# Reordering the opening of a cross-attention and feed-forward kernel: unit-matrix products first, transposes ahead of keys, small pieces between maxima

## The chip, the core and the metric

The kernel runs on one core of a Trainium2 chip. A core has five engines with a queue each: TensorE (matrix products into PSUM; PE in the profile, its weight loads PEld), VectorE (DVE), ScalarE (ACT), GpSimd (POOL) and SyncE (SP, which here only issues transfers). The metric is the time of one execution in microseconds (us) on the device. The kernel before was run three times: 1314.48, 1314.66 and 1316.01 us, median 1314.66. Its traced execution is a further one.

## What is computed

One cross-attention layer and one feed-forward layer, each with a residual. Tokens are 2048 x 256, the context 1601 x 192, 16 heads of 64. A learned null key and value stand ahead of the 1601 context keys, so there are 1602. Cut to what matters:

```python
def xattn(x, context, mask, g_norm, null_kv, Wq, Wkv, Wout, g_out):
    x = layer_norm(x, g_norm)
    q = x @ Wq
    k, v = jnp.split(context @ Wkv, 2, axis=-1)
    # heads split; null key and value put ahead of k and v
    sim = jnp.einsum('bhid,bhjd->bhij', q * sqrt_scale, k * sqrt_scale)
    sim = jnp.where(full_mask, sim, max_neg)
    attn = jax.nn.softmax(sim, axis=-1)
    out = jnp.einsum('bhij,bhjd->bhid', attn, v)
    return layer_norm(heads_joined(out) @ Wout, g_out)

x = x + xattn(layernorm(x), ctx_768, mask, ...)
x = x + ffn(layernorm(x), k0, k1, k2, s0, s1, s2)   # three layers with weights of +1 and -1
```

## The kernel before

Heads are taken in pairs (8 pairs, `p`), tokens in blocks of 512 (4 blocks, `b`); a unit is one pair and one block, and there are 32. A unit needs the queries of its block (`project_q`: `qT` for the scores, `qr` in a rounded format for the maxima), the keys of its pair (`kT`, `kr`), the values (`v`) and, for each query, the largest score over all keys. The maxima of the next unit are found while the exponentials of this one run. Keys are taken in three chunks of 512 and a rest of 66 (`CHUNKS`), tokens of a block in four tiles of 128; `max_chunk` number `3 * t + c` is token tile `t` against key chunk `c`, and number 12 (`REST`) is all four tiles against the rest. Each is a pair of products on TensorE (L338, one for each head; L322 for the rest) and a reduction on VectorE (L341; L325 for the rest).

`max_combined` (L346) joins the maxima of a unit into `mcol`, `max_turned` transposes that on TensorE (L351) and spreads it into `mT` on VectorE (L353). The first two score tiles of a unit add `mT` through a product with ones (L386), so that a unit's first exponential (L388) needs it. After its 13 exponentials a unit does the weighted sums (L395) and the projections for later units.

The change touches the opening (L506 to L550), all that runs ahead of unit 0. It is written out by hand: every engine executes its instructions in the order in which the code issues them. What it does:

- Transfers are issued from three queues: tokens, weights of pair 0 and context on SyncE and ScalarE; mask, null key, `g_norm` (as `gn_sb`) and small things on GpSimd. GpSimd also makes the unit matrix `ident`.
- Block 0 of the tokens is normed: statistics (L77, L78) and a square root (`input_root`), then four tiles scaled on VectorE (`input_normed`, L89).
- `first_keys(n)` projects a key chunk: two products (L214 with the first 128 context rows, L215 with the rest), then VectorE masks it into `kT` (L217) and rounds it into `kr` with the null key put in (L218).
- `input_turned(0)` transposes the normed tiles (eight transposes, L440) and multiplies by `gn_sb`: one half on ScalarE (L441), the other on VectorE (L445).
- Statistics of token block 1 are taken in two parts, around the VectorE work of key chunk 1. Block 1 is normed on ScalarE (`centred_beside`, eight activations), and then the table of the exponential is loaded (L523).
- `project_q(0, 0)`: four passes on TensorE (L203), copies on ScalarE (L204, L205).
- The maxima of unit 0 come in three rounds of four token tiles, one round for each of the key chunks 0, 1 and 2. Between them stand the key chunks 2 and 3, four groups of values (`first_values`, 4, 4, 4 and 1 tiles of 128 keys, two products of two passes each, one copy on ScalarE, L265) and the transposes of block 1.
- `keys_stepped` replaces each 256 keys by the difference to the 256 before, on GpSimd (L251).
- After the last maxima: `max_combined`, the query projection of block 1, `max_turned`.

In the opening, products go to PSUM slots that `slot` hands out, by turns from two pools (`spare` and `flex`) of two slots each. A tile takes over the slot of the tile four calls before it, and waits until that one has been read.

Of the kernel before, what the change touches and what calls it, by code (L numbers as in the profile page):

```python
# [30 lines left out]
REST = 12  # L31
# [5 lines left out]
def xattn_ffn(ctx, tc, x, ctxT, mask, g_norm, null_kv, wq, wkv, wout, g_out, k0, k1, k2, s0, s1, s2, out):  # L37
    nc = tc.nc
# [14 lines left out]
    x_sb = cp.tile([128, NB * 4, D], F32, name="x_sb")  # L53
# [7 lines left out]
    ident = cp.tile([128, 128], F32, name="ident")  # L61
    xnT = cp.tile([128, NB, 2, 512], F32, name="xnT")
# [25 lines left out]
    def centred(dst, src, mv, r, j):  # L88
        nc.vector.tensor_scalar(dst, src, mv[:, j, 0:1], r[:, j : j + 1], ALU.subtract, ALU.mult)  # L89
# [56 lines left out]
    with ExitStack() as att:  # L146
# [20 lines left out]
        weights = {}  # L167
# [26 lines left out]
                pp.tile([128, KEYS], F32R, tag="kr", name=f"kr_{p}"),  # L194
            )

        def project_q(p, b, get=flex):

            qT = wp.tile([128, 512], F32, tag="qT", name=f"qT_{p}_{b}")
            qr = wp.tile([128, 512], F32R, tag="qr", name=f"qr_{p}_{b}", bufs=1)  # L200
            ps = get(f"psq_{p}_{b}")
            for c in range(2):
                nc.tensor.matmul(ps[:, 0, :], weights[p][0][:, c, :], xnT[:, b, c, :], start=c == 0, stop=c == 1)  # L203
            nc.scalar.mul(qr, ps[:, 0, :], DH**-0.5)  # L204
            nc.scalar.mul(qT, ps[:, 0, :], DH**-0.5)  # L205
            queries[p, b] = (qT, qr)

        def first_keys(n, get):

            kT, _, kr = pairs[0]  # L210
            start, w = CHUNKS[n]
            keys = ds(start, w)
            ps = get(f"psk_0_{n}")
            nc.tensor.matmul(ps[:, 0, :w], weights[0][1][:, 0, :], ctx_a[:, keys], start=True, stop=False)  # L214
            nc.tensor.matmul(ps[:, 0, :w], weights[0][2][:, 0, :], ctx_b[:, keys], start=False, stop=True)  # L215

            nc.vector.tensor_tensor(kT[:, keys], ps[:, 0, :w], keep[:, keys], ALU.mult)  # L217
            nc.vector.scalar_tensor_tensor(kr[:, keys], drop[:, keys], nullk[:, 0:1], kT[:, keys], ALU.mult, ALU.add)  # L218
            if n == 0:
                nc.vector.tensor_copy(kT[:, 0:1], nullk)  # L220
# [25 lines left out]
        def keys_stepped(p):  # L246

            kT = pairs[p][0]
            for at in range(256 * ((KEYS - 1) // 256), 0, -256):
                w = min(256, KEYS - at)  # L250
                nc.gpsimd.tensor_tensor(kT[:, ds(at, w)], kT[:, ds(at, w)], kT[:, ds(at - 256, w)], ALU.subtract)  # L251

        def first_values(n, get):

            v = pairs[0][1]
            tiles = range(4 * n, min(4 * n + 4, KC))
            rows = 128 if n < 3 else KLAST
            ps = get(f"psv_0_{n}")
            for i, t in enumerate(tiles):
                keys = ds(128 * t, rows)  # L260
                out_t = ps[:rows, 0, ts(i, 128)]
                nc.tensor.matmul(out_t, ctx_a[:, keys], weights[0][1][:, 1, :], start=True, stop=False)
                nc.tensor.matmul(out_t, ctx_b[:, keys], weights[0][2][:, 1, :], start=False, stop=True)
            w = len(tiles)
            nc.scalar.copy(  # L265
                v[:rows, ds(4 * n, w), :], ps[:rows, 0, : 128 * w].rearrange("p (t d) -> p t d", d=128)
            )
            if n == 0:
                nc.gpsimd.tensor_copy(v[0:1, 0, :], nullv)
# [149 lines left out]

        def input_root(b, mv=None):
            mv = mv or stats(x_sb[:, ts(b, 4), :], 4, f"x{b}")
# [12 lines left out]
        def input_turned(b, get=flex):  # L436
            pt = get(f"xT_{b}")
            for j in range(4):
                for c in range(2):
                    nc.tensor.transpose(pt[:, c, ts(j, 128)], y_sb[:, 4 * b + j, ts(c, 128)], ident)  # L440
            nc.scalar.mul(xnT[:, b, 0, :], pt[:, 0, :], gn_sb[:, 0:1])  # L441
            if b == 1:
                nc.scalar.mul(xnT[:, b, 1, :], pt[:, 1, :], gn_sb[:, 1:2])
            else:
                nc.vector.tensor_scalar_mul(xnT[:, b, 1, :], pt[:, 1, :], gn_sb[:, 1:2])  # L445
# [63 lines left out]
        xn = input_root(0)  # L509

        for keys in (ds(0, 512), ds(512, KEYS - 512)):
            nc.scalar.activation(drop[:, keys], keep[:, keys], AF.Identity, bias=ones[:, 0:1], scale=-1.0)
        input_normed(0, *xn)
        first_keys(0, slot)
        input_turned(0, slot)
        mv = stats(x_sb[:, 4:6, :], 2, "x1")
        first_keys(1, slot)
        mv = stats(x_sb[:, 6:8, :], 2, "x1", mv)
        xn = input_root(1, mv)
        project_q(0, 0, slot)  # L520
        input_normed(1, *xn, beside=True)

        nc.scalar.activation(warm, eps_sb, AF.Exp)  # L523
        for t in range(4):
            max_chunk(0, 0, 3 * t, slot)
            if t == 1:
                first_keys(2, slot)
        for t in range(4):
            max_chunk(0, 0, 3 * t + 1, slot)
            if t == 0:  # L530
                first_keys(3, slot)
                keys_stepped(0)
            else:
                first_values(t - 1, slot) if t < 3 else input_turned(1, slot)

        nc.vector.tensor_scalar(maskb[:, : KC - 1], mcol_u8[:, : KC - 1], -MASKED, MASKED, ALU.mult, ALU.add)
        nc.vector.tensor_scalar(
            maskb[:KLAST, KC - 1 : KC], mcol_u8[:KLAST, KC - 1 : KC], -MASKED, MASKED, ALU.mult, ALU.add
        )
        for t in range(4):  # L540
            max_chunk(0, 0, 3 * t + 2, slot)
            if t == 0:
                max_chunk(0, 0, REST, slot)
            if t == 1:
                first_values(2, slot)
            if t == 2:
                first_values(3, slot)
        max_combined(0, 0)
        project_q(0, 1, flex)
        max_turned(0, 0)  # L550
        begin.__exit__(None, None, None)
        last = None
# [256 lines left out]
```

## Time and profile before

| what | value |
|---|---|
| median of three runs | 1314.66 us |
| the profiled execution | 1314.12 us |
| its span, first to last instruction | 1312.3 us |
| TensorE busy in it | 1288.0 us (98%) |
| VectorE busy | 820.1 us (62%) |
| ScalarE busy | 625.3 us (48%) |
| GpSimd busy | 998.9 us (76%) |
| mean granted TensorE clock | 0.993 |
| first reduction of a maximum starts | 20.45 us |
| last maxima joined (L346) starts | 41.58 us |
| `mT` (L353) starts | 43.14 us |
| first exponential (L388) starts | 44.43 us |

Times inside the profile are us from the start of the span. Busy time counts an engine's instructions, except register, branch, semaphore and transfer-issuing ones. An idle time in square brackets is followed by what ended it, inferred from semaphore events; "issue" is time for which the profile shows no such event. An fp32 product is two passes on TensorE, and the counts behind an "x" are passes. The ends of products are modelled, so the start of the next pass tells more than a duration. "PEclk" is the granted clock of TensorE as a share of full speed (on the page in tenths).

### The profile page before, as it was taken

To read this page: it belongs to the slowest core of one execution; us is meant where nothing else is said; L and a number is where in the kernel's file an instruction comes from. 1 tells how busy PE (TensorE), PEld (TensorE's weight loads), DVE (VectorE), ACT (ScalarE), POOL (GpSimd) and SP (SyncE) were. 2 spreads that over 40 slices of the span, in tenths; PEclk is the share of its full clock that TensorE was granted. 3 is DMA by queue.
4 is the path that set the end of the run, shared out by engine and by line. 5 is a ranking of instruction groups with operands and counts; after the bars stand their busy time and mean duration, and the time that the engine had idled before them with its cause. 6 is when DMAs were issued, how large, how long until landed. Compare 5 with 4: busy or idle time off the path is not lost.

```text
span 1312.3 us, 15885 instructions
## 1 busy us (share of the span) xinstructions
PE 1288.0 (98%) x6528; PEld 654.4 (50%) x6528; DVE 820.1 (62%) x822; ACT 625.3 (48%) x740; POOL 998.9 (76%) x503
## 2 busy tenths in 40 slices
PE   6989999999999999999999999999999999999998
PEld 3434444444444444444444444444444443688887
DVE  6877666666666666666666666666666784554431
ACT  3566444444444445455555555555555457421121
POOL 3578988898889888898889888988898999611100
PEclk8989999999999999999999999999999999999999
DMA  6100000000000000000000000000000010000000
GB/s 142 22 1 4 0 1 13 5 1 0 12 5 1 1 13 1 4 1 1 13 5 0 0 13 5 0 1 4 0 17 1 0 41 0 1 9 8 17 16 16
DMA packets 16121, 13.16 MB, mean 10 GB/s; under 512 B 2656, under 2 KB 15520, under 8 KB 16048
## 3 DMA queue, kind: packets, MB, share of 16 engines
q1 hardware_dynamic: 14928, 11.02, 3.2%
q8 instruction: 51, 0.84, 0.3%
q0 software_dynamic: 480, 0.34, 0.2%
q10 hardware_dynamic: 640, 0.79, 0.2%
q14 instruction: 22, 0.18, 0.0%
HBM read 10.04 MB, written 2.10 MB: 9 GB/s over the span
## 4 chain that ended last, share of the span: by engine, by line
PE 92%; DVE 3%; ACT 2%; POOL 2%; issue 1%; DVEq 0%; POOLq 0%; ACTq 0%
PE sT L375 28%; PE av L395 26%; PE ps L693 9%; PE max L338 7%; PE psq L203 4%; PE po L403 4%; PE ps L719 2%; PE den L413 2%; PE psv L280 2%; PE psk L228 1%; PE sT L386 1%; DVE mx L341 1%; POOL acc L596 1%; PE psv L292 1%; PE psk L233 1%; PE max L322 1%
## 5 line engine op out<-in xcount | busy, mean ns | idle before, releaser
L596 POOL TENSOR_TENSOR acc<-acc,e 128x1024 f32<-128x1024 f32 (+1 forms) x352 | 847.4, 2407 | 27.6
L341 DVE TENSOR_REDUCE mx<-max 128x2 f32<-128x1024 f32 x384 | 452.0, 1222 | 84.1 <-PE max L338 84.0
L388 ACT ACTIVATE e<-sT,maskb 128x1024 f32<-128x1024 f32 (+1 forms) x416 | 460.1, 1115 | 39.4 <-PE sT L386 8.8
L375 PE MATMUL sT<-qT,kT 64*128 64x512 f32 (+1 forms) x1664 | 449.6, 612 | 0.8 <-ACT e L388 0.2
L395 PE MATMUL av<-e,v 128*64 128x512 f32 (+1 forms) x1664 | 369.5, 594 | 0.2 <-ACT e L388 0.2
L338 PE MATMUL max<-kr,qr 64*128 64x512 f32 x768 | 292.3, 751 | 3.2 <-ACT qr L204 2.3
L395 PEld LDWEIGHTS av<-e,v 128*64 128x64 f32 (+1 forms) x1664 | 116.7, 137 | 237.7 <-issue 223.2
L375 PEld LDWEIGHTS sT<-qT,kT 64*128 64x128 f32 (+1 forms) x1664 | 130.7, 181 | 153.4 <-ACT e L388 144.4
L644 ACT COPY avs<-av 128x512 f32<-128x512 f32 x32 | 18.7, 586 | 321.6 <-PE av L395 321.6
L415 DVE RECIPROCAL aoT<-den 128x512 f32<-128x512 f32 x31 | 104.1, 3357 | 59.9 <-PE den L413 59.9
L594 POOL TENSOR_TENSOR acc<-e,e 128x1024 f32<-128x1024 f32 x32 | 75.6, 2363 | 71.0 <-ACT seen L584 57.8
L338 PEld LDWEIGHTS max<-kr,qr 64*128 64x128 f32 x768 | 76.3, 187 | 93.8 <-DVE mx L341 69.4
L353 DVE TENSOR_TENSOR mT<-mt,pick 128x512 fp32r<-128x512 f32 x32 | 22.1, 691 | 119.1 <-PE mt L351 119.1
L693 PE MATMUL ps<-h0hi,w 128*128 128x512 f32 x256 | 79.6, 392 | 0.1
L693 PE MATMUL ps<-h0lo,w 128*128 128x512 f32 x256 | 78.9, 389 | 0.0
L122 POOL TENSOR_TENSOR y_sb<-y_sb,gout_sb 128x256 f32<-128x256 f32 x12 | 9.3, 777 | 88.8 <-DVE y_sb L89 88.8
L204 ACT ACTIVATE qr<-psq 128x512 fp32r<-128x512 f32 x32 | 19.1, 597 | 97.4 <-PE psq L203 97.4
L203 PE MATMUL psq<-xnT,wq 128*128 128x512 f32 x128 | 62.0, 608 | 2.5 <-DVE xnT L445 2.5
L682 DVE SCALAR_TENSOR_TENSOR h1lo<-ps,h1hi 128x1024 fp32r<-128x1024 f32 x16 | 19.6, 1224 | 68.3 <-ACT h1hi L681 68.2
L681 ACT ACTIVATE h1hi<-ps 128x1024 fp32r<-128x1024 f32 x16 | 16.4, 1026 | 94.9 <-PE ps L693 94.9
L403 PE MATMUL po<-wo,aoT 128*128 128x256 f32 x256 | 60.6, 379 | 0.0
L251 POOL TENSOR_TENSOR kT<-kT 128x256 f32<-128x256 f32 (+1 forms) x48 | 31.8, 662 | 36.0 <-DVE kr L240 17.5
(153 smaller groups left out, 1075.6 us busy)
## 6 DMA issues: line engine op xcount, KB each, us to landing
out_x<-o SPq DMA_DIRECT2D x7, 256.0 KB, 2.1
x_sb<-in_x SPq DMA_DIRECT2D x3, 512.0 KB, 8.4
wa<-in_wkv SPq DMA_DIRECT2D x8, 128.0 KB, 2.7
wq<-in_wq SPq DMA_DIRECT2D x8, 128.0 KB, 2.2
wo<-in_wout SPq DMA_DIRECT2D x8, 128.0 KB, 2.1
xnT<-in_k SPq DMA_DIRECT2D x1, 1024.0 KB, 5.8
wb<-in_wkv SPq DMA_DIRECT2D x15, 64.0 KB, 2.4
ctx_a<-in_ctxT SPq DMA_DIRECT2D x2, 256.0 KB, 8.8
```

The lines of the kernel that those rows point to most:

```text
L203: nc.tensor.matmul(ps[:, 0, :], weights[p][0][:, c, :], xnT[:, b, c, :], start=c == 0, stop=c == 1)
L251: nc.gpsimd.tensor_tensor(kT[:, ds(at, w)], kT[:, ds(at, w)], kT[:, ds(at - 256, w)], ALU.subtract)
L338: nc.tensor.matmul(ps[:, j, :w], qr[rows, ts(t, 128)], kr[rows, ds(start, w)], start=True, stop=True)
L341: nc.vector.tensor_reduce(maxima[p, b][:, t, :, c], ps[:, :, :w], AX.X, ALU.max)
L375: nc.tensor.matmul(ps[:n, j, :], kT[rows, ds(128 * k, n)], qT[rows, :], start=k < 2, stop=k >= 2, skip_group_check=k >= 2,)
L388: nc.scalar.activation(e[:n], ps[:n], AF.Exp, bias=maskb[:n, k : k + 1])
L395: nc.tensor.matmul(av[ts(j, DH), 0, :], v[:n, k, ts(j, DH)], e[:n, j, :], start=k == 0, stop=k == KC - 1)
L403: nc.tensor.matmul(pv[:, t, :], aoT[:, ts(t, 128)], weights[p][3], start=True, stop=True)
L415: nc.vector.reciprocal(aoT, ps)
L594: nc.gpsimd.tensor_tensor(acc, es[0], es[1], ALU.add)
L596: nc.gpsimd.tensor_tensor(acc[:m], acc[:m], es[k][:m], ALU.add)
L693: nc.tensor.matmul(ps[:, f, :], w(c)[:, ts(2 * g + f, 128)], parts[part][:, c, :], start=i == 0, stop=i == len(steps) - 1,)
```

## The change

All of it is in the opening; the unit loop and the feed-forward part are as they were.

1. Behind the norming of block 0, twenty products of `ident` with itself go to a PSUM tile `idle` that nobody reads. They are the first work on TensorE.
2. The transposes of block 0 (`input_turned(0)`) come ahead of key chunk 0, the query projection of block 0 ahead of key chunk 1. On VectorE, L445 is thus ahead of the first keys.
3. The statistics of block 1 are no longer split: all four tiles are taken behind the first keys and ahead of the VectorE work of key chunk 1. `input_root` loses its second argument.
4. `first_values` takes a `part`: two of a group's four tiles in each call, the copy behind the second. `project_q` can be called in two parts, too, one product in each.
5. The maxima stand in the same three rounds, but between two of them at most one small piece is placed: half a group of values, a key chunk, the transposes of block 1, or half of the query projection of block 1. That projection now stands ahead of `max_combined`, its first half ahead of chunk 8 and its second behind chunk 11, and it takes its PSUM tile from `slot` instead of `flex`.

The order of TensorE's work from key chunk 1 on, before: max 0, 3, keys 2, max 6, 9, 1, keys 3, max 4, values 0, max 7, values 1, max 10, transposes of block 1, max 2, rest, 5, values 2, max 8, values 3, max 11, first scores, query 1, turned maxima. After: max 0, 3, keys 2, max 6, half of values 0, max 9, the other half, max 1, keys 3, half of values 1, max 4, the other half, max 7, transposes of block 1, max 10, half of values 2, max 2, the other half, rest, values 3, max 5, half of query 1, max 8, 11, the other half, first scores, turned maxima. The order of GpSimd's and SyncE's work and of all transfers is the same, but for the copy of the null value, which now stands ahead of `keys_stepped` on GpSimd.

```diff
-        def project_q(p, b, get=flex):
-
+        def project_q(p, b, get=flex, part=None):
+
+            if part is not None:
+                if part == 0:
+                    halves["q"] = get(f"psq_{p}_{b}")
+                ps = halves["q"]
+                nc.tensor.matmul(
+                    ps[:, 0, :], weights[p][0][:, part, :], xnT[:, b, part, :], start=part == 0, stop=part == 1
+                )
+                if part == 0:
+                    return
...
-        def first_values(n, get):
+        def first_values(n, part, get):
...
-            ps = get(f"psv_0_{n}")
+            if part == 0:
+                halves[n] = get(f"psv_0_{n}")
+            ps = halves[n]
             for i, t in enumerate(tiles):
+                if i // 2 != part:
+                    continue
...
             w = len(tiles)
+            if part == 0 and w > 1:
+                return
...
         input_normed(0, *xn)
+
+        idle = slot("idle")
+        for _ in range(20):
+            nc.tensor.matmul(idle[:, 0, :128], ident, ident, start=True, stop=True)
+        input_turned(0, slot)
         first_keys(0, slot)
-        input_turned(0, slot)
-        mv = stats(x_sb[:, 4:6, :], 2, "x1")
+        project_q(0, 0, slot)
+        xn = input_root(1)
         first_keys(1, slot)
-        mv = stats(x_sb[:, 6:8, :], 2, "x1", mv)
-        xn = input_root(1, mv)
-        project_q(0, 0, slot)
         input_normed(1, *xn, beside=True)
 
         nc.scalar.activation(warm, eps_sb, AF.Exp)
-        for t in range(4):
-            max_chunk(0, 0, 3 * t, slot)
-            if t == 1:
-                first_keys(2, slot)
-        for t in range(4):
-            max_chunk(0, 0, 3 * t + 1, slot)
-            if t == 0:
-                first_keys(3, slot)
-                keys_stepped(0)
-            else:
-                first_values(t - 1, slot) if t < 3 else input_turned(1, slot)
+
+        max_chunk(0, 0, 0, slot)
+        max_chunk(0, 0, 3, slot)
+        first_keys(2, slot)
+        max_chunk(0, 0, 6, slot)
+        first_values(0, 0, slot)
+        max_chunk(0, 0, 9, slot)
+        first_values(0, 1, slot)
+        max_chunk(0, 0, 1, slot)
+        first_keys(3, slot)
+        keys_stepped(0)
+        first_values(1, 0, slot)
+        max_chunk(0, 0, 4, slot)
+        first_values(1, 1, slot)
+        max_chunk(0, 0, 7, slot)
+        input_turned(1, slot)
+        max_chunk(0, 0, 10, slot)
...
-        for t in range(4):
-            max_chunk(0, 0, 3 * t + 2, slot)
-            if t == 0:
-                max_chunk(0, 0, REST, slot)
-            if t == 1:
-                first_values(2, slot)
-            if t == 2:
-                first_values(3, slot)
+        first_values(2, 0, slot)
+        max_chunk(0, 0, 2, slot)
+        first_values(2, 1, slot)
+        max_chunk(0, 0, REST, slot)
+        first_values(3, 0, slot)
+        max_chunk(0, 0, 5, slot)
+        project_q(0, 1, slot, 0)
+        max_chunk(0, 0, 8, slot)
+        max_chunk(0, 0, 11, slot)
+        project_q(0, 1, slot, 1)
         max_combined(0, 0)
-        project_q(0, 1, flex)
         max_turned(0, 0)
```

More of the change, by code (lines that the diff above doesn't have):

```diff
@@ L195, in open_pair @@
             )
-        def project_q(p, b, get=flex):
+        def project_q(p, b, get=flex, part=None):
[8 more added lines that the diff above has]
+                    return
             qT = wp.tile([128, 512], F32, tag="qT", name=f"qT_{p}_{b}")
             qr = wp.tile([128, 512], F32R, tag="qr", name=f"qr_{p}_{b}", bufs=1)
-            ps = get(f"psq_{p}_{b}")
-            for c in range(2):
+            if part is None:
+                ps = get(f"psq_{p}_{b}")
+            for c in range(2) if part is None else ():
                 nc.tensor.matmul(ps[:, 0, :], weights[p][0][:, c, :], xnT[:, b, c, :], start=c == 0, stop=c == 1)
@@ L251, in keys_stepped @@
                 nc.gpsimd.tensor_tensor(kT[:, ds(at, w)], kT[:, ds(at, w)], kT[:, ds(at - 256, w)], ALU.subtract)
-        def first_values(n, get):
+        halves = {}
+        def first_values(n, part, get):
             v = pairs[0][1]
@@ L417, in divided, with input_root @@
             return aoT
-        def input_root(b, mv=None):
-            mv = mv or stats(x_sb[:, ts(b, 4), :], 4, f"x{b}")
+        def input_root(b):
+            mv = stats(x_sb[:, ts(b, 4), :], 4, f"x{b}")
             r = sp.tile([128, 4], F32, tag="rstd", name=f"rstd_x{b}")
```

## The prediction

> **What bounds the kernel now.** First the page: the chain of work that ended last, followed back from the end, and the granted clock.
>
> ```profile
> PEclk8989999999999999999999999999999999999999
> PE 92%; DVE 3%; ACT 2%; POOL 2%; issue 1%; DVEq 0%; POOLq 0%; ACTq 0%
> ```
>
> Over the whole span TensorE sets the end. The change edits only the opening, and there another engine may bind, so the opening is read alone. It ends where the first shifts (mT, L353) let the first exponentials start, at 44.4 us. The table of busy time by stretch comes next (length, then busy us of PE, PEld, DVE, ACT, POOL, the clock, DMA share, GB/s).
>
> ```profile
> 20.45:41.58 21.13, 19.29 (x102) 13.04 (x101) 16.67 (x19) 8.29 (x16) 4.19 (x7) 0.84 0.08 16
> 41.58:44.43 2.85, 2.85 (x11) 1.20 (x11) 0.88 (x2) 1.09 (x3) 0.00 (x0) 1.00 0.89 200
> ```
>
> The first stretch runs from the first maximum to the last. VectorE has 16.67 us of work in 21.13 us: 4.46 us idle. VectorE's timeline says what it waited for.
>
> ```profile
> 12.39 0.69 DVE L217 TENSOR_TENSOR kT<-psk,keep 128x512 f32<-128x512 f32 x1 [3.64 <-issue]
> ...
> 14.76 0.75 DVE L445 TENSOR_SCALAR xnT<-xT,gn_sb 128x512 f32<-128x512 f32 x1 [0.64 <-ACT xnT L441]
> ...
> 20.45 2.36 DVE L341 TENSOR_REDUCE mx<-max 128x2 f32<-128x1024 f32 x2 [0.81 <-PE max L338]
> 23.95 0.69 DVE L217 TENSOR_TENSOR kT<-psk,keep 128x512 f32<-128x512 f32 x1 [1.15 <-PE psk L215]
> ...
> 31.91 1.23 DVE L341 TENSOR_REDUCE mx<-max 128x2 f32<-128x1024 f32 x1 [1.49 <-PE max L338]
> 34.33 1.23 DVE L341 TENSOR_REDUCE mx<-max 128x2 f32<-128x1024 f32 x1 [1.19 <-PE max L338]
> ...
> 41.58 0.19 DVE L346 TENSOR_REDUCE mcol<-mx 128x8 f32<-128x32 f32 x1
> 43.14 0.69 DVE L353 TENSOR_TENSOR mT<-mt,pick 128x512 fp32r<-128x512 f32 x1 [1.37 <-PE mt L351]
> ```
>
> Each idle stretch ends with a TensorE product that came late: a key chunk at 23.95, maxima at 31.91 and 34.33 that stood behind whole groups of values, the turned maxima at 43.14 that stood behind a query projection (40.94 to 42.76). Why TensorE was late is in the chain of the opening (start, us, what) and in its clock.
>
> ```profile
> 10.59 1.71 PE psk L215 x2
> ...
> 29.31 0.43 PE psv L263 x2
> ...
> 33.18 0.22 PE psv L263 x2
> 17.65:21.06 3.41, 1.16 (x5) 1.00 1.13 288
> 21.06:24.50 3.44, 3.44 (x8) 0.51 0.08 22
> 24.50:27.88 3.38, 1.80 (x13) 1.00 0.00 0
> 27.88:31.30 3.42, 3.42 (x16) 0.50 0.00 0
> ```
>
> The same two passes take 0.43 us at clock 0.5 and 0.22 us at 1.0. The clock fell at 21.06 and 27.88, after stretches in which TensorE was busy 1.16 and 1.80 of 3.4 us, and came back after stretches in which it was always busy. (The column reads 1.00 before 21 us, yet the key chunk at 10.59 takes 1.71 us where its like at 14.87 takes 0.86, so I go by durations there.)
>
> The last view is the landing of two transfers, issued at 3.68 and 5.46 us; the last number is us to landing.
>
> ```profile
> gn_sb<-in_g_norm POOLq DMA_DIRECT2D x1, 1.0 KB, 7.8
> x_sb<-in_x SPq DMA_DIRECT2D x1, 512.0 KB, 9.2
> ```
>
> So gn_sb lands at 11.5 (GpSimd's own wait on it ends at 11.79) and the second token block at 14.66. No transfer is moved by the change, so these times stand.
>
> **The change part by part.** *Unit-matrix products.* Twenty fp32 products of 128 columns wait for ident alone, which is ready at 2.64 us. A value tile's two products are four passes and take 0.43 us at half clock, so twenty take 20 x 0.215 = 4.3 us and end at 6.9. The transposes queued behind them need the first normed tile, at 7.38 + 0.41 = 7.8. The cover is 0.9 us; with twice the passes the burst would end near 11.2, the transposes at 12.9, and the loss would be about 1.1 us. What they gain I take as nothing: after the burst TensorE has eight transposes and one key chunk, then waits for gn_sb, so by 12 us it can be at half clock again, and nothing that the clock speeds up before 12 us is waited for.
>
> *Transposes ahead of keys.* They follow the normed tiles and end near 9.2 (before: 13.8). Their readers (L441 on ScalarE, L445 on VectorE) gain a new limit, gn_sb. I take GpSimd's 11.79 rather than 11.5: ScalarE then copies 11.8 to 12.5, VectorE starts at 12.5. Behind L445 on VectorE stand the first keys, the statistics of block 1 and all maxima; behind L441 on ScalarE stands qr. The first key chunk needs wb (issued 1.95, landing 7.6 us later, 9.55) and at half clock ends by 11.3; VectorE asks for it at 13.2: hidden. The query's second half starts at 13.25, ends by 14.1 at half clock, and key chunk 1 by 15.8; VectorE asks for it at 17.05: hidden. Key chunk 2 waits for its transfers (8.42 + 8.4 = 16.8), ends by 18.5, and is asked for at 20.9: hidden.
>
> *VectorE's queue, added up from 12.5.* L445 0.67 (14.76 to 15.43); first keys and null column 1.72 (12.39 to 14.11), which gives 14.89, past the landing at 14.66; four statistics of 0.54 (two take 15.43 to 16.51) give 17.05; keys 1, 1.36 (16.51 to 17.87), give 18.41; reciprocal and negated mean 0.24 (19.40 to 19.64) give 18.65. The first maximum, at 20.45 before, thus starts 1.8 us earlier. From there the work is the same 16.67 us: 35.3 if VectorE never waits, against 41.58.
>
> *Values, keys, queries between chunks.* The PSUM slots are four, taken in turn. A maximum costs VectorE 1.14 us (2.36 for two, overlapping). Between two maxima TensorE has one pair of products, 0.43 us, and one piece of some 0.43 us: 0.87 at full clock, inside 1.14; 1.3 to 1.7 at half clock, outside it. Two places are thin. The first copy of values stands on ScalarE behind eight norming steps and a table load (3.9 + 1.5 us, from 18.65 to 24.1), ends at 24.7 and frees the slot of the second values; the maximum behind them is ready by 26.0 and asked for at 26.25. Then eight transposes of block 1 (1.04 us at full clock, 1.7 at half) stand ahead of chunk 10: ready by 28.0 at full clock, 29.5 at half, asked for at 28.5. So VectorE waits 0 to 1 us there; if nothing improved it would keep all 4.46 us. I take 0.5, near the low end, since no whole group of values stands ahead of a maximum any more. [...]
>
> *Query 1 between the last chunks.* Half of it now stands ahead of chunk 8, the rest behind chunk 11, while VectorE still reduces. The turned maxima then wait for mcol alone: 0.19 + some 0.08 + 0.38 (42.76 to 43.14) = 0.65 us from L346 to L353, against 1.56: 0.9 saved.
>
> *Entry to unit 0.* TensorE is idle about 2 us of the last 3.4 before mT, so the clock may fall as it did at 21.06. A scoring step takes 1.17 us and holds 0.70 us of TensorE work (47.09 to 47.54 scores, 0.25 maxima): 1.4 at half clock, so three steps lose 0.7 us at most, 0 at least. I take 0.2.
>
> Sum: -1.8 - 4.46 + 0.5 - 0.91 + 0.2 = -6.5 us. The units behind it have no fixed time left to wait for (the last opening transfers land at about 20 us, and the reload of ctx_b follows the last values), so it reaches the end whole. The profiled execution took 1314.12 us, of which the span is 1312.3: 1307.6. The median of the runs lies 0.5 above the profiled one: 1308.1, given as 1308.
>
> **The rivals.** *The maxima still wait.* The slots of two engines' readers keep VectorE idle for the old 4.46 us. For it: the two thin places. Against it: the waits of before each had a whole group of values or a key chunk ahead of them. Gain 1.8 + 0.9 = 2.7: 1312.0.
>
> *Absorbed behind the opening.* Unit 0 ends with the norming of block 2, after which TensorE stood idle 2.70 us (72.93); were that bound to something other than unit 0's maxima, nothing would be left: 1314.7. Against it: the statistics there start at 67.05, right behind VectorE's unit-0 work.
>
> *Slower: a clock that stays at half.* If the fall at the entry to unit 0 lasted the unit, thirteen steps would lose 0.23 each (1.4 - 1.17), 3.0 us, and the weighted sums (58.85 to 70.2) would double, 11.4 us: +14.4 - 6.7 = +7.7, 1322. It decides once the clock is still low some 4 us into the weighted sums. Against it: both falls in the trace ended after one busy stretch of 3.4 us. [...]
>
> **How the numbers follow.** The forecast gets 0.81 (its own range 1305.6 to 1310.5: no waits and a lucky clock at 72 to 83 us, where a query projection took 3.64 against 1.98 us, to 2 us more waits). The waiting rival gets 0.09, half of it on either side of the bound, the absorbed one 0.05, the stuck clock 0.05. About 0.2%, 2.6 us, can be told from no change. Faster is then 0.81 + 0.05 = 0.86, same 0.09, slower 0.05. The range is 1305.5 to 1311.5: it reaches into the waiting case and leaves out the rest.
>
> **What would show it.** Right: xnT on ScalarE starting at 11.5 to 11.8, the first maximum at 18.5 to 18.8, less than 1.5 us of VectorE idle until L346's successor at 35.3 to 36.3, mT 0.7 us behind it, and a granted clock that is low again before 12 us. Wrong: xnT waiting on TensorE, a VectorE wait of over 1 us on a maximum, a first exponential later than 39 us, or a half clock lasting into unit 0's weighted sums.

## The result and the profile after

| | before | after |
|---|---|---|
| median (range) of six runs each, same chip | 1314.58 us (1313.49 to 1316.11) | 1309.98 us (1309.12 to 1310.28) |
| traced execution / its span | 1314.12 / 1312.3 us | 1309.90 / 1308.1 us |
| first maximum starts | 20.45 us | 18.08 us |
| last maxima joined | 41.58 us | 36.78 us |
| `mT` starts | 43.14 us | 37.92 us |
| first exponential of unit 0 | 44.43 us | 39.21 us |
| first exponential of unit 1 | 86.18 us | 81.99 us |

After takes 0.9969 of the time before, 95% interval 0.9959 to 0.9979. The gain is 4.6 us between the medians and 4.2 us between the two spans. The forecast was 6.5.

The page of after first: the granted clock by slices of the span, and the shares of the chain that ended last.

```profile
PEclk9989999999999999999999999999999999999999
...
PE 91%; DVE 3%; ACT 2%; POOL 2%; DMA 1%; issue 1%; SPq 0%; DVEq 0%; POOLq 0%; ACTq 0%
```

TensorE still sets the end. The line of before has two dips of the clock, in the first slice (0 to 33 us, the opening) and in the third (66 to 98 us, the passage from unit 0 to unit 1). The first is gone in after, the second is there in both. The new share of DMA is the head: the chain now runs through the two token transfers, the second of which landed at 14.4 us.

The table of busy time by stretch, from the first maximum of after to the last (columns as before):

```profile
18.08:36.78 18.70, 17.14 (x101) 10.79 (x100) 16.95 (x22) 9.48 (x18) 4.23 (x7) 1.00 0.33 77
```

The clock was full in all of it, where it was 0.84 before. VectorE is busy 16.95 of 18.70 us. It still stands idle for some 1.8 us (4.46 before), and VectorE's timeline of after tells where.

```profile
11.75 0.75 DVE L463 TENSOR_SCALAR xnT<-xT,gn_sb 128x512 f32<-128x512 f32 x1 [2.88 <-ACT xnT L459]
...
18.08 2.35 DVE L359 TENSOR_REDUCE mx<-max 128x2 f32<-128x1024 f32 x2
...
27.26 1.23 DVE L359 TENSOR_REDUCE mx<-max 128x2 f32<-128x1024 f32 x1 [0.29 <-PE max L356]
28.70 1.23 DVE L359 TENSOR_REDUCE mx<-max 128x2 f32<-128x1024 f32 x1 [0.22 <-PE max L356]
...
31.88 0.71 DVE L343 TENSOR_REDUCE mx<-max 128x8 f32<-128x528 f32 x1 [0.43 <-PE max L340]
32.90 1.23 DVE L359 TENSOR_REDUCE mx<-max 128x2 f32<-128x1024 f32 x1 [0.30 <-PE max L356]
34.39 2.36 DVE L359 TENSOR_REDUCE mx<-max 128x2 f32<-128x1024 f32 x2 [0.27 <-PE max L356]
36.78 0.19 DVE L364 TENSOR_REDUCE mcol<-mx 128x8 f32<-128x32 f32 x1
37.92 0.69 DVE L371 TENSOR_TENSOR mT<-mt,pick 128x512 fp32r<-128x512 f32 x1 [0.96 <-PE mt L369]
```

The waits of 1.15, 1.49, 1.19 and 0.44 us have become five of 0.22 to 0.43. They come one behind another from 27 to 34 us: not two accidents, but one engine that is slower than the other throughout. The chain of waits of after names it (start, us, what).

```profile
22.08 1.28 ACT L543
23.36 0.01 issue
23.38 0.20 ACT warm L543
23.58 0.48 ACT v L283
...
24.11 0.49 PE psv L278 x2
24.59 0.22 PE psv L279 x2
24.82 0.22 PE psv L278 x2
25.04 0.22 PE psv L279 x2
25.27 0.43 PE max L356
25.69 0.42 PE psv L278 x2
```

From 24.11 to 34.36 us the chain never leaves TensorE. Half a group of values (four products of two passes each) takes from 24.11 to 25.27, 1.16 us at full clock, and the maxima behind it 0.43. Together that is some 1.5 us for each reduction that costs VectorE 1.14. The chain enters TensorE from the first copy of values, which stands on ScalarE behind the table load (L543).

Where the span's 4.2 us come from: the first maximum starts 2.37 us earlier; the way from there to the joined maxima is 18.70 us instead of 21.13 (2.43); from there to `mT` 1.14 instead of 1.56 (0.42); from `mT` to the first exponential 1.29 in both. That makes 5.22 at unit 0. From unit 0's to unit 1's first exponential, however, after takes 42.78 us and before 41.75: 1.03 us are given back, 4.19 remain. The timeline of TensorE in after shows the place.

```profile
73.90 3.78 PE L213 MATMUL psq<-xnT,wq 128*128 128x512 f32 x4 [2.46 <-DVE xnT L463]
77.47 2.45 PE L238 MATMUL psk<-ctx_a,wa 128*128 128x401 f32 x4
```

These are the projections between unit 0 and unit 1, at half clock (0.50 from 69.12 to 79.36 us). The same four passes of keys (x4) in before:

```profile
82.60 1.51 PE L228 MATMUL psk<-ctx_a,wa 128*128 128x401 f32 x4
```

There the clock was 0.50 from 72.25 to 82.49 us, so that it had come back 38.06 us after unit 0's first exponential; in after it took 40.15. What stood behind it was tested below.

### The profile page after: what moved, and what is told of

The parts are those of the page before. It is cut to its first block, busy times and chain, and to the rows that moved or that the text cites. A ratio compares the mean times of both kernels' runs of the same rounds, so it can differ in the third digit from the quotient of the medians.

```text
span 1308.1 us, 15963 instructions
## 1 busy us (share of the span) xinstructions
PE 1290.2 (99%) x6568; PEld 657.8 (50%) x6568; DVE 819.7 (63%) x822; ACT 624.7 (48%) x740; POOL 997.9 (76%) x503
## 4 chain that ended last, share of the span: by engine, by line
PE 91%; DVE 3%; ACT 2%; POOL 2%; DMA 1%; issue 1%; SPq 0%; DVEq 0%; POOLq 0%; ACTq 0%
PE sT L393 28%; PE av L413 26%; PE ps L720 9%; PE max L356 7%; PE psq L213 4%; PE po L421 4%; PE ps L746 2%; PE den L431 2%; PE psv L298 2%; PE psk L238 2%; PE sT L404 1%; DVE mx L359 1%; POOL acc L623 1%; PE psv L310 1%; DMA x_sb<-in_x 1%; PE psk L243 1%
## 5 line engine op out<-in xcount | busy, mean ns | idle before, releaser
L404 PE MATMUL sT<-mT,ones_r 64*128 64x512 f32 x128 | 52.3, 787 | 1.3 <-DVE mT L371 1.3
```

Of the source, the lines that this page charges most:

```text
L404: nc.tensor.matmul(ps[:n, j, :], ones_r[rows, :n], mT[rows, :], start=False, stop=True)
```

## The experiments

Medians are given with their range; the kernel before ran beside each on the same chip. Over all these runs it lay between 1310.5 and 1316.8 us, so a single run of it says little.

### Without the unit-matrix products

```diff
-        idle = slot("idle")
-        for _ in range(20):
-            nc.tensor.matmul(idle[:, 0, :128], ident, ident, start=True, stop=True)
+        n_slots += 1
```

> The changed kernel without the twenty unit-matrix products, all else as it is. Order theory (the prediction's: nothing that the clock speeds up before 12 us is waited for): the key chunk, queries and maxima up to 18 us have slack of 1 us and more on VectorE's side even at half clock, so the first reduction still starts at 18.0 to 18.6 and the median is within 0.7 us of the changed kernel's 1310.0. Clock theory: the changed kernel's clock stayed at full speed through the whole opening because the burst had raised it; without it the values between the maxima (0.43 us a product at half clock, 0.22 at full) meet half clock for one window or two of 3.4 us, mT comes 1.5 to 4 us later, and the median is 1311.5 to 1314.

Measured: 1309.66 us (1309.31 to 1311.23), ratio to before 0.9971 (0.9961 to 0.9981), the same as after. In its TensorE timeline the head of the queue:

```profile
7.82 1.94 PE L458 MATMUL xT<-ident,y_sb 128*128 128x128 f32 x8 [7.82 <-DVE y_sb L89]
...
14.58 1.02 PE L224 MATMUL psk<-ctx_a,wa 128*128 128x512 f32 x2
```

The transposes start 1.8 us earlier than in after (9.62, behind the burst) and take 1.94 us instead of 1.04. Both end before `gn_sb` lands (the line that replaces the burst keeps the turns of the PSUM slots as they are); the first maximum starts at 18.34 us, the way to the joined maxima is 18.68. The burst is worth nothing: the maxima are as fast without it. One thing was not expected: the clock fell at the entry to unit 0 (0.52 from 40 to 42 us), where the third exponential started 4.30 us behind the first instead of 2.64, 1.66 us lost; yet unit 1 began at 81.56, no later than in after.

### The burst alone, on the kernel before

```diff
         input_normed(0, *xn)
+        idle = spare("idle")
+        for _ in range(20):
+            nc.tensor.matmul(idle[:, 0, :128], ident, ident, start=True, stop=True)
         first_keys(0, slot)
```

> The kernel before with the twenty unit-matrix products put ahead of its first key chunk, order of all else as before. Order theory: the burst brings less than 1 us, 1313.6 to 1314.6. Clock theory: the two stretches at half clock (21.06 to 24.50, 27.88 to 31.30) shrink or vanish, the reductions at 23.95, 31.91 and 34.33 wait less, and 2 us or more of the 4.6 us are there already: 1310.5 to 1312.5.

Measured: 1313.34 us (1310.70 to 1314.89, 12 runs), ratio 0.9997 (0.9989 to 1.0006). The first maximum starts at 20.04 us, `mT` at 43.36 (before: 43.14). The clock fell twice in the opening (0.50 from 18 to 24 us and from 28 to 30), as it had before. Alone, too, the burst is worth nothing.

### The head alone, with the old order behind it

```diff
         input_turned(0, slot)
         first_keys(0, slot)
         project_q(0, 0, slot)
...
-        max_chunk(0, 0, 6, slot)
-        first_values(0, 0, slot)
-        max_chunk(0, 0, 9, slot)
-        first_values(0, 1, slot)
+        for t in range(4):
+            max_chunk(0, 0, 3 * t + 1, slot)
...
         max_combined(0, 0)
+        project_q(0, 1, flex)
         max_turned(0, 0)
```

> The changed kernel's burst and head (transposes ahead of keys, query ahead of key chunk 1, statistics in one piece) with the maxima, values and query 1 in the order of before. The first reduction should start at 18.1 as in the changed kernel. Order theory: the small pieces between the maxima bring most of the rest, so this one is at 1312 to 1313. Rival (TensorE is bound by its own work between 24 and 34 us even at full clock, since a half group of values costs it 0.87 us and not the 0.43 of the prediction): the pieces only move the same TensorE work about, and this one is at 1310 to 1311.5, the query's early half being the rest.

The burst's tile comes from `spare` directly here, which shifts the turns of `slot` by one.

Measured: 1311.95 us (1310.91 to 1313.30, 11 runs), ratio 0.9989 (0.9981 to 0.9998). The first maximum starts at 18.46 us, the way to the joined maxima takes 20.18 and from there to `mT` 1.99. VectorE's timeline has the old waits again:

```profile
28.98 1.23 DVE L359 TENSOR_REDUCE mx<-max 128x2 f32<-128x1024 f32 x1 [1.80 <-PE max L356]
...
31.39 1.23 DVE L359 TENSOR_REDUCE mx<-max 128x2 f32<-128x1024 f32 x1 [1.18 <-PE max L356]
```

The median lies at the edge of what the order theory expected, outside the rival's range. The change has two gains that add. The head starts the maxima some 2 us earlier, and the small pieces shorten the way through them by 1.5 (20.18 against 18.70). Part of that 1.5 is the clock: with the old order it was 0.50 from 22 to 28 us, so that the wait of 1.80 fell into half clock; the one of 1.18, behind a whole group at full clock, did not.

### The table load later

The chain of after enters TensorE through the copy behind the table load, so the load was moved behind the transposes of block 1.

```diff
-        nc.scalar.activation(warm, eps_sb, AF.Exp)
...
         input_turned(1, slot)
+        nc.scalar.activation(warm, eps_sb, AF.Exp)
         max_chunk(0, 0, 10, slot)
```

> The changed kernel with the load of the exponential table moved from behind the norming of block 1 to behind its transposes, so that the copy of the first values on ScalarE no longer stands behind it. If the chain of the changed kernel reads right (copy of values at 23.48 behind the load, TensorE without a gap from 24.11 on), the copy ends 1.3 us earlier, TensorE fills its wait before 24.11, mT comes about 1.2 us earlier, and the median is 1308.5 to 1309.2. If VectorE or the slots bind, it stays at 1309.8 to 1310.3.

Measured: 1310.20 us (1308.73 to 1310.56), ratio 0.9971 (0.9960 to 0.9982): no gain over after. Yet the first copy of values moved from 23.48 to 22.13 us, the way through the maxima fell from 18.70 to 18.04 and `mT` came at 37.28, 0.64 earlier. The gain went right behind that. ScalarE's timeline, and the busy time by stretch:

```profile
38.57 1.11 ACT L406 ACTIVATE e<-sT,maskb 128x1024 f32<-128x1024 f32 x1 [2.45 <-PE sT L404]
40.54 1.11 ACT L406 ACTIVATE e<-sT,maskb 128x1024 f32<-128x1024 f32 x1 [0.86 <-PE sT L404]
42.86 12.78 ACT L406 ACTIVATE e<-sT,maskb 128x1024 f32<-128x1024 f32 x11 [1.21 <-PE sT L393]
```

```profile
35.60:39.00 3.40, 1.73 (x11) 0.83 (x9) 1.58 (x4) 0.95 (x3) 0.00 (x0) 1.00 0.11 28
39.00:42.40 3.40, 3.40 (x20) 2.26 (x16) 1.74 (x2) 1.79 (x2) 0.67 (x1) 0.51 0.00 0
```

In the 3.4 us in which the last maxima are joined and turned, TensorE is busy 1.73 us. Behind it the clock is 0.51 for 3.4 us, and the third exponential starts 4.29 us behind the first instead of 2.64. Earlier by 0.64, then later by 1.65: the load is on the path, and the clock at the entry decides whether that shows. The one run with a mean granted clock of 0.996 took 1308.73 us; the five at 0.995, the traced one among them, took 1310.11 to 1310.56.

### The query projection back behind the joined maxima

```diff
-        project_q(0, 1, slot, 0)
         max_chunk(0, 0, 8, slot)
         max_chunk(0, 0, 11, slot)
-        project_q(0, 1, slot, 1)
         max_combined(0, 0)
+        project_q(0, 1, flex)
         max_turned(0, 0)
```

> The changed kernel with the query projection of block 1 whole and behind the joined maxima, as it was before. TensorE-bound theory: the 1.7 us of this projection stood in TensorE's unbroken stretch from 24 to 35.6 us, so taking it out lets the last maximum be read about 1.5 us earlier (mcol at 35.3 instead of 36.78), but the turned maxima then wait for the projection (1.56 us from mcol to mT, as before the change, against 1.14): mT at 36.9, some 1 us earlier than 37.92, the first exponential at 38 to 38.5. The prediction's view (VectorE binds, the early projection saves 0.9): mT 0.4 us later than in the changed kernel, the first exponential at 39.5 or later. The median within 1 us of 1310 either way, since the clock at the next boundary can give or take 1 us.

Here, too, the burst's tile comes from `spare` directly.

Measured: 1309.70 us (1309.45 to 1310.63), ratio 0.9961 (0.9949 to 0.9973). From the joined maxima to `mT` it takes 1.56 us again, as before, against 1.14; but the way to the joined maxima is 18.35 instead of 18.70. From the first maximum to `mT` that is 19.91 against 19.84. Neither number that was expected came. Since TensorE is behind in the maxima anyway, a query projection moved in between them costs there nearly what it saves behind them (0.35 against 0.42).

### The clock kept up between unit 0 and unit 1

To test the 1.03 us given back, unit products fill TensorE's gaps there, in after and in before.

```diff
+                if u == 0:
+                    fill = spare("fill")
+                    for _ in range(24):
+                        nc.tensor.matmul(fill[:, 0, :128], ident, ident, start=True, stop=True)
                 if u < 2:
                     input_turned(u + 2)
                 if nxt is not None:
                     max_turned(*nxt)
+                if u == 0:
+                    for _ in range(10):
+                        nc.tensor.matmul(fill[:, 0, :128], ident, ident, start=True, stop=True)
```

> The changed kernel with 24 unit-matrix products behind unit 0's weighted sums (where TensorE stands idle 2.7 us waiting for the normed tiles) and 10 behind the turned maxima (idle 2.5 us). Theory: the gain of the opening is part lost here, since TensorE's clock falls to half in the idle time and comes back only at the end of a busy window; with the clock kept up the query projection takes 1.9 us and not 3.8, the key projection 1.5 and not 2.5, so the first exponential of unit 1 starts about 2.7 us earlier, and the median is 1306.8 to 1308. Rival: the products come back no faster, or they delay the transposes, 1309.5 to 1311.

Measured on after: 1307.79 us (1307.36 to 1309.30), ratio 0.9947 (0.9936 to 0.9959). The projections in its TensorE timeline:

```profile
74.56 1.98 PE L213 MATMUL psq<-xnT,wq 128*128 128x512 f32 x4
76.39 1.51 PE L238 MATMUL psk<-ctx_a,wa 128*128 128x401 f32 x4
```

1.98 and 1.51 us instead of 3.78 and 2.45, and 40.07 us between the two first exponentials instead of 42.78. The granted clock is 1.00 from 64 to 80 us, where after has 0.50 from 70 to 78. There it fell at 69.12, while TensorE stood idle between two transposes, and came back at 79.36, behind 5.46 us in which TensorE was always busy.

> The kernel before with the same 24 and 10 unit-matrix products at the same place. It takes the clock of this boundary out of the comparison. If the change's opening gain of 5.2 us is real and 1 us of it was lost to the clock at the boundary, this kernel is 5 us or a little more slower than the changed kernel with the same products: 1312 to 1313.5, and 1.5 to 2 us faster than the kernel before. If the loss had another cause, the two differ by 4.2 us as without the products.

Measured on before: 1312.35 us (1308.97 to 1314.03, 12 runs), ratio 0.9982 (0.9972 to 0.9991). Between the first exponentials it takes 40.09 us, the same as with the fill on after, and the clock is 1.00 from 64 to 82 us. So with the clock held up, the 5.3 us that the opening gains here (45.21 to 39.89) reach the end whole: the two spans are 1311.5 and 1306.1. The medians differ by only 4.56; with the kernel before and this one spread over 4 to 5 us from run to run they cannot tell 4.2 from 5.3, so the size of what was given back rests on the traces.

The granted clocks of the single runs tell more. A stretch of 3.4 us at half clock lowers the mean clock of a run by 0.0013 (half of 3.41 us in 1310). Of the twelve runs of before with the fill, one has a mean of 1.000, so no such stretch, and took 1308.97 us; the other eleven, at 0.995 to 0.999, took 1310.62 to 1314.03 (the traced one, with two falls in its opening, 1313.28). The five runs of after with both fillings (next section), all at 1.000, took 1307.21 to 1307.97. With no fall in either, the change would thus be worth only some 1.3 us. Most of the 5.3 would then be time that the opening of before loses to falls of its clock, and that the new order saves by leaving no such gaps on TensorE. One run without a trace is behind this, so it is a strong hint and not shown.

### The clock kept up at the entry, too

The fill, and five unit products behind `max_turned(0, 0)`:

```diff
         max_turned(0, 0)
+        entry = flex("entry")
+        for _ in range(5):
+            nc.tensor.matmul(entry[:, 0, :128], ident, ident, start=True, stop=True)
```

> As the changed kernel with the 24 and 10 products at the boundary, and five more between the turned maxima and the product that spreads mT, where TensorE is idle for 1.26 us ahead of unit 0. Theory: the clock no longer falls at the entry to unit 0 (the variant without the burst and the one with the late table lost 1.7 us and 1.7 us there, the traced changed kernel nothing), so this is the same as without the five where that one does not fall, up to 1.5 us faster where it does: 1306.5 to 1307.8 with less spread over runs. Rival: the five delay mT's product, +0.5 us.

Measured: 1307.68 us (1307.21 to 1307.97), ratio 0.9944 (0.9932 to 0.9956). The median is that of the fill alone to 0.1 us (the clock had held at the entry in the traces of after and of the fill alone, too: 1.00, with the third exponential 2.64 us behind the first in all three); the runs now lie within 0.8 us.

### Half the products of values, first without and then with a filling

If TensorE's amount of work makes the maxima wait, halving the values must end the waits. The second product of each value tile is left out.

```diff
-                nc.tensor.matmul(out_t, ctx_a[:, keys], weights[0][1][:, 1, :], start=True, stop=False)
-                nc.tensor.matmul(out_t, ctx_b[:, keys], weights[0][2][:, 1, :], start=False, stop=True)
+                nc.tensor.matmul(out_t, ctx_a[:, keys], weights[0][1][:, 1, :], start=True, stop=True)
```

> The changed kernel with the second of each value tile's two products left out in the opening (the last 64 of the 192 context rows are missing from pair 0's values): 13 products of 0.22 us less on TensorE, 2.9 us in all, with everything else as it is. TensorE-bound theory: VectorE's waits of 0.2 to 0.4 us before each maximum from 27 us on go, from the first reduction to mcol it takes 16.9 to 17.3 us and not 18.7, and mT comes 1.4 to 1.8 us earlier. VectorE- or slot-bound (the prediction's sum): still 18.4 to 18.7 us. The median may keep less of it, since the clock at the entry to unit 0 and at its end gives and takes 1 to 2 us.

Measured: 1310.27 us (1308.60 to 1312.15), ratio 0.9971 (0.9959 to 0.9983). From the first maximum to the joined maxima it took 19.33 us, longer than with twice the products. Both theories missed. The busy time by stretch says why:

```profile
21.00:24.40 3.40, 2.19 (x12) 1.51 (x12) 3.36 (x5) 3.32 (x7) 0.00 (x0) 0.95 0.23 47
24.40:27.80 3.40, 3.17 (x12) 2.19 (x11) 2.94 (x5) 0.43 (x1) 1.40 (x4) 0.50 0.45 122
27.80:31.20 3.40, 3.40 (x14) 0.54 0.01 4
```

With the work gone, TensorE was busy 2.19 us in the first of these stretches. Its clock of 0.95 says that the fall came just inside it, at 24.09 us; in the 3.41 us ahead of that TensorE was busy 2.04. From there to some 30.9 us, for 6.8 us, the clock was then at half (0.50, and 0.54 with the end of it). So the same kernel was given eight unit products in the first two halves of values, three and five, to keep TensorE busy there:

```diff
+            for _ in range((3, 5)[part] if n == 0 else 0):
+                nc.tensor.matmul(ps[:, 1, :128], ident, ident, start=True, stop=True)
```

> The kernel with half of the value products left out again (pair 0's values lack the last 64 context rows), and eight unit-matrix products put where TensorE then stood idle ahead of 24 us, in an unread part of the first values' PSUM tile, so that the clock does not fall at 24 us as it did in the traced execution without them. TensorE-bound theory: with the clock up, the waits of 0.2 to 0.4 us before the maxima from 27 us on shrink, and from the first reduction to mcol it takes 16.9 to 17.6 us (18.70 in the changed kernel, 19.33 with the fallen clock). VectorE- or slot-bound: 18.4 to 18.7 us. If the clock falls all the same, no verdict.

Measured: 1309.28 us (1307.88 to 1309.70), ratio 0.9957 (0.9941 to 0.9972). VectorE's timeline:

```profile
26.43 3.48 DVE L360 TENSOR_REDUCE mx<-max 128x2 f32<-128x1024 f32 x3
...
31.89 3.68 DVE L360 TENSOR_REDUCE mx<-max 128x2 f32<-128x1024 f32 x3
35.60 0.19 DVE L365 TENSOR_REDUCE mcol<-mx 128x8 f32<-128x32 f32 x1
```

No row of it has a wait left: from the first maximum, at 18.93, to the joined ones it takes 16.67 us, as much as VectorE's work there in before, and the clock is 1.00 in all of it. So in after the maxima wait for the amount of TensorE's work on values, at full clock. (At the entry to unit 0 the clock then fell, to 0.50 from 38 to 40 us: `mT` came at 36.76, 1.16 us earlier than in after, but the third exponential at 42.31, 0.46 later, 3.97 us behind the first instead of 2.64.)

### After once more, and all that helped together

After unchanged, and after with both fillings and the later table load.

> The changed kernel unchanged, for a comparison within one set of runs: 1309.1 to 1310.3, as before. [...]

Measured: 1309.99 us (1309.70 to 1311.37), ratio 0.9970 (0.9959 to 0.9982). The first maximum starts at 18.63 us here, half a microsecond later than in the first trace, as the second token block landed that much later (VectorE's wait for it ends at 14.99 instead of 14.44); the way to the joined maxima is 18.68 us.

> The late table load together with the products that keep the clock up at the entry to unit 0 (5) and at its end (24 and 10). The late load alone brought mT 0.64 us earlier and lost it again at a fallen clock at the entry. If that reading holds, the opening's 0.6 us now reaches the end: 1306.9 to 1307.3, against 1307.7 for the same kernel with the early load. If it does not, 1307.5 to 1308.

Measured: 1306.85 us (1306.49 to 1307.33), ratio 0.9944 (0.9930 to 0.9958). It beats both kernels; beside after on the same chip (1309.70 to 1311.37) the ranges do not touch. The table of busy time by stretch, at the passage to unit 1 and to be held against the clock of 0.72 that the same stretch had in after:

```profile
64.00:82.00 18.00, 17.89 (x127) 13.20 (x123) 11.49 (x14) 11.15 (x21) 10.40 (x6) 1.00 0.00 1
```

With the clock held up, the later table load, which alone showed nothing, now counts: 0.8 us between the medians of this kernel and of both fillings alone. These were measured on different chips, and their ranges overlap by 0.1 us; the traces agree, with 18.05 us from the first maximum to the joined ones against 18.69.

## Why the prediction was right, and where not

The forecast of 1308.0 us was 2.0 too low; the measured 1309.98 is inside its range, and the direction and the mechanism held: an earlier head, then fewer waits in the maxima. Three of the terms below came out much worse, though, and it is luck that a head better than forecast made up for a part. VectorE's idle time (1.8 us), the joined maxima (36.78 us) and `mT` (1.14 us behind them) missed what the prediction had named as signs of being right, and one of its signs of being wrong came: a first exponential later than 39 us (39.21). The terms of its sum:

| term | forecast | traces |
|---|---|---|
| first maximum earlier | 1.8 | 2.37 (18.08 us; 1.8 in the second trace of after, 18.63) |
| VectorE's waits left in the maxima | 0.5 | 2.0 (18.70 less the 16.67 of the forecast; 1.8 by the 16.95 of after's own row) |
| joined maxima to `mT` | 0.65 | 1.14 |
| entry to unit 0 | 0.2 lost | 0 in after, 1.3 to 1.7 where the clock fell |
| reaching the end | whole | 1.03 given back at unit 1 |

*The head.* The step was right, and so was its limit, the transfer of `gn_sb`. In after, ScalarE's timeline has:

```profile
11.03 0.69 ACT L459 ACTIVATE xnT<-xT,gn_sb 128x512 f32<-128x512 f32 x1 [1.84 <-DMA gn_sb<-in_g_norm]
```

The product with `gn_sb` waited for that transfer, not for TensorE, and started 0.8 us earlier than the 11.79 that I had taken. VectorE thus had its first keys behind it by 14.14 us, and the last wait of the head was another: 0.30 us for the second token block, landed at 14.44, where I had the queue go on at 14.89. In the second trace of after that wait ended at 14.99. Between executions these landings differ by as much as my error.

*The burst* came to nothing, as forecast, but not by my working. "A value tile's two products are four passes and take 0.43 us at half clock" is wrong: the row that I read, x2 passes in 0.43 us at half clock, is one product. One unit product costs 0.43 us at half clock and 0.22 at full, so the burst took not 4.3 us but 7.0:

```profile
2.70 7.09 PE L535 MATMUL idle<-ident 128*128 128x128 f32 x40 [2.70 <-POOL ident masks.py:199]
...
9.62 1.04 PE L458 MATMUL xT<-ident,y_sb 128*128 128x128 f32 x8
```

The cover of 0.9 us was gone: the transposes stood behind the burst for 1.8 us. They ended at 10.66 us all the same, 0.4 us ahead of `gn_sb`. That was luck: the prediction had named this case ("with twice the passes") and put its loss at 1.1 us, by half clock throughout, but TensorE went faster while the burst ran (15 passes from 2.7 to 6.0 us, 27 from 6.0 to 9.6), and the transposes took 1.04 us. Wrong as well: "by 12 us it can be at half clock again". A key product took 0.86 us (10.50 to 11.36), and the clock read 1.00 from then to 69.12 us, behind the end of unit 0.

*The maxima: the step that failed.* The prediction has "one piece of some 0.43 us: 0.87 at full clock, inside 1.14". The same misreading halved the piece: half a group of values is four products, eight passes, 0.87 us even back to back at full clock and 1.1 to 1.16 as traced, and with the maxima's 0.43 some 1.5 us. That is outside 1.14 without any fall of the clock. Hence waits of 0.2 to 0.4 us all along in place of the two thin places I looked for; the kernel with half the products, its clock kept up, ran the 16.67 us that I had forecast for "never waits". The thin place at the table load is real (moving the load brought `mT` 0.64 us earlier), but it is where the chain enters TensorE, not what keeps it there. The rival in which VectorE keeps all 4.46 us fell: 2.4 us of it went, with the new order and the clock that stayed full under it. The sum counted the waits of before without asking how much of them was the clock; by the one run of before with the fill whose clock stayed full, much of it was.

*Joined maxima to `mT`.* I took 0.38 us from the start of the transpose's product in before, and left out its weight load, which there ran beside the query projection's last pass (load at 42.33, product at 42.76). From that load to `mT` it is 0.81 us in before and 0.84 in after (37.08 to 37.92); of the latter the chain of waits has 0.45 us as "issue", for which the profile shows no cause. Moving the projection gained 0.42 us there, and putting it back showed that the maxima lose nearly as much.

*Entry and passage.* That what the opening gains "reaches the end whole" holds only with the clock the same. The fall at the entry did not happen in after's traces and happened in four others, where the third exponential came 1.3 to 1.7 us late and not "0.7 us at most": with TensorE late, the scoring steps lose more than I had counted. And in after the clock came back later after unit 0's first exponential than in before (40.15 us against 38.06). The range allowed for a lucky clock at 72 to 83 us only, and the sum for neither. Of the two other rivals, the absorbed gain came true for 1.03 us, by the clock, and a clock stuck at half through unit 0 was seen in no trace. The argument against the latter overlooked a fall: in before's trace the one between the units lasted from 72.25 to 82.49 us, 10.24 us and not 3.4.

## What to carry to other kernels

Before a piece is fitted between two others, count its passes against a row whose count is known to be one instruction; a factor of two in the unit turned "fits" into "does not fit". When a reorder moves less than its trace terms promise, look at the granted clock behind the moved stretch: gaps that open on TensorE can cost more than the work saved (here 19.33 us against 18.70 with half the products of values). And before a gain is put down to the order, compare runs of equal granted clock: a good part of it may be gaps that closed (here some 1.3 us were left between runs with a mean clock of 1.000, by one run of before). In these runs a handful of idle products in known gaps cost nothing that could be seen, held the clock (a mean of 1.000 in all five runs with both fillings), and made another gain show (0.8 us).

## What was not expected of the hardware

TensorE's clock fell here without a long idle time. It fell at 39.03 us in the run with the later table load, behind a stretch of 3.4 us in which TensorE was busy for 1.73 us, with gaps of 0.42 and 1.25 us, and at 24.09 us in the run with half the values, behind 3.41 us of which it was busy for even 2.04. No bound follows: in after it was busy for only 1.73 of the 3.41 us from 35.26 to 38.67, and the clock read 1.00 there and until 69.12. In the run with half the values a stretch busy for 3.17 of 3.40 us did not bring the clock back (0.50), and in the next one, always busy, it came back at some 30.9 us. In the run without the burst the query projection from 74.78 us on took 3.37 us, against 3.78 at half clock in after, from which I estimate that the clock came back at about 77.6, with TensorE idle for some 0.6 of the 3.4 us before. So these traces give no rule for the way back. Taking work out of TensorE thus made the maxima slower: 19.33 us against 18.70 with half the products of values.

The start of unit 1 hardly followed the opening: it lay between 81.6 and 82.3 us in the six traces without the filling between the units whose unit 0 began at 38.34 to 39.80 us. Why was not shown. The clock came back at 78.5 to 79.4 us in the four of them in which it was read there, and at about 77.6 and 80.0 in the other two, by my estimate from the lengths of their projections (queries 3.37 us and keys 2.76, against 3.78 and 2.45 in after). Holding the clock up took both the loss and most of the spread away: 1307.2 to 1308.0 us with both fillings, against 1310.5 to 1316.8 for the kernel before.
